# A cross-attention and LoRA-expert kernel: the second tile of the next pair turned in the second joint product instead of in the middle of the third

## The chip, the cores and the metric

The kernel runs on one core of a Trainium2 chip. The metric is the device time of one execution in microseconds (us), as the median of several executions. In the text, PE is the tensor engine, PEld its loads of stationary weights, DVE the vector engine, ACT the scalar engine, POOL the GpSimd engine and SP the sync engine, whose queue issues all DMAs here. PSUM is the memory that PE writes its products to; it is handed out in banks of 128 partitions by 512 float32 numbers.

## The reference

All data are float32. There are 8 batches of 1024 rows, each of 1024 numbers. Two layers follow one another, each with a residual:

```python
# layer 1: attention of layernorm(x) to 64 context rows, masked
scores = einsum('bsd,bmd->bsm', layernorm(x), ctx) / sqrt(1024)
scores = where(mask[:, None, :], scores, -1e30)
readout = einsum('bsm,bmd->bsd', softmax(scores), ctx)
x = x + where(any(mask), readout, 0)
# layer 2: a dense 1024x1024 layer plus 8 low-rank experts, two of them per row
h = layernorm(x)
base = einsum('btd,od->bto', h, weight)
probs = softmax(einsum('btd,ed->bte', h, router_w))
w_dense = the two largest probs of each row, scaled to sum 1, zero elsewhere
Ax = einsum('nd,erd->ner', h, lora_A)                # rank 16
expert_out = einsum('ner,ne,eor->no', Ax, w_dense, lora_B) * 2.0
x = x + base + expert_out
```

## The kernel before

**Tiles and pairs.** A tile is 128 rows of x, so there are 64 tiles and 32 pairs of tiles. Pair u holds tiles r = 0 and r = 1 in `xts[u]`. After `first()`, which does the start and pairs 0 and 1, the function `quad(u)` (L973) is called 15 times, for u = 2, 4, ..., 30. One call does the dense layer and the experts for pairs u and v = u + 1, the second part of the attention for n = u + 2 and m = u + 3 and the first part for f = u + 4. `more` is true while pair n exists (14 calls), `far` while pair f exists (13 calls).

**Turned rows.** For the matmuls the normalised rows h have to stand with their columns on the partitions. `f_rows(u)` (L264) makes h with ACT from two small DVE results; `norm_send` writes it to DRAM (`hd<-h`), `norm_fetch` reads it back in a blocked order into two tiles `hs` (`hs<-hd`), and `rt_turn_tile(u, r)` (L491) turns one of them on DVE, in two instructions of 128x512: one into `hA` (`has[u]`) and one into `hB` (`hbs[u]`). `rt_turn(u)` (L498) does this for r = 0 and r = 1. The tiles `xs`, `xT`, `h` and `hs` share one ring of six buffers (L64).

**Products with fewer multiplications.** The dense layer of a pair is a two-by-two product of blocks (two tiles by two halves of the 1024 columns), done with seven block products and sums of blocks, in the manner of Strassen and Winograd. Four of the seven, numbered 1, 6, 7 and 8, accumulate in one bank (`product`). The other three and a fourth are taken for two pairs at once as "joint" products 5, 3, 2 and 4 (`joint`, L692), each again done with seven smaller products, on quarters of 256 columns. The sums of blocks that these need are made on DVE by `joint_sums`, in two halves `one` and `two`, for joints 5 and 3 together and for joints 2 and 4 together.

**One joint product.** It uses two banks, `jl` (lower: the halves p4 and chain) and `ju` (upper: p2 and p5). PE fills a half bank with a block of four matmuls, DVE adds it to x (`part`, `to_x`; both are line 714 of the profile), and where PE then accumulates further into that half bank it has to wait for DVE's read. The middle of it:

```python
        block(p5, s1, q1, True)          # PE
        part(v, 1, p5)                   # DVE reads p5
        hook(4)
        block(chain, s2, q2, False)      # PE
        part(u, 1, chain)                # DVE reads chain
        hook(5)
        block(p5, s4, b22, False)        # PE goes on in p5
        low(u, p5, 1)
        hook(6)
        block(chain, s3, q3, False)      # PE goes on in chain
        part(v, 0, chain)
```

**Order.** The order of the instructions on PE, DVE, ACT and SP is written by hand: each engine works through its instructions in the order in which the Python code calls them. `hooks` are lists of functions that `joint` calls between its steps, so that other work lies between the blocks. `quad` runs joint 5, 3, 2, 4 at its end. In joint 3, step 2 holds `att_rstd` and `att_exp` of pair f, step 5 `rt_turn(n)` and step 7 `att_divide(f)`. Before joint 2 comes `one` of the sums for joints 2 and 4. In joint 2, step 1 holds `end_3` (the last lora product and add of joint 3) and `f_rows(m)`, step 2 holds `two`, and step 3 `att_turn_p(f)`. In joint 4, step 1 holds `rows_0` (the end of joint 2, stores, `norm_fetch(m)` and a load), and step 5 `rt_sums(n)`, which reads `hA` and `hB` of both tiles of pair n.

Of the kernel before, what the change touches and what calls it, by code (L numbers as in the profile page):

```python
# [24 lines left out]
def kernel(  # L25
# [61 lines left out]
    def transpose_blocked(dst, src):  # L87

        nc.vector.transpose(  # L89
            dst.rearrange("p k (t i) -> p t k i", i=NB),  # L90
            src.rearrange("p t (k i) -> p t k i", i=NB),
        )
# [171 lines left out]
    def f_rows(u: int, fetch: bool = True):  # L264

        nm, std = fts.pop(u)
        rstd = small.tile([P, 2, 1], F32, tag="rstdf", name=f"rstdf_{u}")
        nc.vector.reciprocal(rstd, std)
        nmr = small.tile([P, 2, 1], F32, tag="nmrf", name=f"nmrf_{u}")
        tt(nmr, nm, rstd, ALU.mult)  # L270
        for r in range(2):
            h = ring.tile([P, D], F32, tag="ring", name=f"h_{u}_{r}")
            hss.setdefault(u, []).append(h)
            nc.scalar.activation(  # L274
                h, xts[u][r], AF.Identity, bias=nmr[:, r, :], scale=rstd[:, r, :]
            )
        norm_send(u, fetch)
# [100 lines left out]
    def att_sc(u: int):  # L378
        sc = ps_at.tile([P, 2, M], F32, tag="at", name=f"sc_{u}")
        nc.tensor.transpose(sc.rearrange("p j m -> p (j m)"), scs.pop(u), ident)  # L380
        scs[u] = sc
# [82 lines left out]
    def norm_send(u: int, fetch: bool = True):  # L464

        hds[u] = dram.tile([2 * P, D], F32, tag="hd", name=f"hd_{u}")
        hs_in, hss[u] = hss[u], []
        for r in range(2):
            nc.sync.dma_start(out=hds[u][r * P : (r + 1) * P, :], in_=hs_in[r])
        if fetch:  # L470
            norm_fetch(u)
# [10 lines left out]
    def h_tiles(u: int):  # L482
        has[u] = turned.tile([P, 2, KH, P], F32, tag="hA", name=f"hA_{u}")
        hbs[u] = turned.tile([P, 2, KH, P], F32, tag="hB", name=f"hB_{u}", bufs=3)
# [6 lines left out]
    def rt_turn_tile(u: int, r: int):  # L491
        if r == 0:
            h_tiles(u)
        half = KH * NB
        for t, c in ((has[u], 0), (hbs[u], half)):
            transpose_blocked(t[:, r], hss[u][r][:, :, c : c + half])

    def rt_turn(u: int):  # L498
        for r in range(2):
            rt_turn_tile(u, r)  # L500
# [6 lines left out]
    def rt_low_rank_tile(u: int, r: int):  # L507
        if r == 0:
            pas[u] = ps_rt.tile([P, 2, ER + E], F32, tag="rt", name=f"pa_{u}")
        pa = pas[u]  # L510
        for k in range(KD):
            h = (has[u] if k < KH else hbs[u])[:, r, k % KH, :]
            mm(pa[:, r, :], h, art_sb[:, k, :], start=(k == 0), stop=(k == KD - 1))  # L513
        if r == 1:
            axls[u] = small.tile([P, 2, ER + E], F32, tag="axl", name=f"axl_{u}", bufs=1)
            nc.scalar.copy(axls[u], pas.pop(u))
# [121 lines left out]
    def product(u: int, i: int, between=None, after: int = 0):  # L638

        if i == 1:  # L640
            pps[u] = bank_of(f"b5_{u}") if u < 2 else None, bank_of(f"ch_{u}")
        b5, chain = pps[u]
        if i == 1:
            block(chain, has[u][:, 0], w11, True, between, after)
        elif i == 5:
            block(b5, sms[u][:, 0], t1, True, between, after)
        elif i == 6:
            block(chain, sss[u][1], t2, False, between, after)
        elif i == 7:
            block(chain, sss[u][2], t3, False, between, after)  # L650
        else:
            lora(u, chain, 1, HB, HB)

    def product_add(u: int, i: int):
        b5, chain = pps[u]
        if i == 5:
            add(u, b5, 1, 1)
            add(u, b5, 0, 1)
        else:
            add(u, chain, *{1: (0, 0), 6: (0, 1), 7: (1, 0), 8: (1, 1)}[i])  # L660
# [312 lines left out]
    def quad(u: int):  # L973

        v, n, m, f = [u + i for i in range(1, 5)]
        more = n < NP
        far = f < NP
        b = f // PPB
        new_mem = far and f % PPB == 0

        product(u, 1, (lambda: att_sc(n)) if u == 2 else None, 1)
        pending.pop()()
        product_add(u, 1)
        rt_low_rank_tile(u, 0)
        rt_turn(v)
        product(u, 6)
        if more:
            x_stats(m)
        if u == 2:
            att_divide(n)  # L990
            att_turn_p(n)
        if more:
            att_turn(m)
        product_add(u, 6)
        if u == 2:
            quarter_sums("t4", t4)
        if new_mem:
            mask_bias(b)
            send_mem(b)
        if far:  # L1000
            load_xs(f)
            load_xt(f)
        rt_low_rank_tile(u, 1)
        product(u, 7)
        rt_top(u)
        product_add(u, 7)
        if more:
            att_readout(n)
            att_scores(m)
            rt_turn_low_rank(u)  # L1010
            att_add(n)

        if more:
            product(v, 1, {0: lambda: att_sc(m), 2: lambda: product(u, 8)})
            att_rstd(m)
            att_exp(m)
            one, two = rt_sums_steps(v)
            one()
            product_add(u, 8)
            product_add(v, 1)  # L1020
            two()
            f_sums(n)
            att_divide(m)
            rt_low_rank_tile(v, 0)
            product(v, 6, lambda: att_turn_p(m), 1)
            f_squares(n)
        else:
            rt_sums(v)
            product(v, 1, {0: lambda: rt_turn_low_rank(u), 2: lambda: product(u, 8)})
            product_add(u, 8)  # L1030
            product_add(v, 1)
            rt_low_rank_tile(v, 0)
            product(v, 6)
        if far:
            att_turn(f)
        product_add(v, 6)
        rt_low_rank_tile(v, 1)
        product(v, 7)
        if new_mem:
            turn_mem(b)  # L1040
        rt_top(v)
        if more:
            f_std(n)
            f_rows(n)
        product_add(v, 7)
        one, two = joint_sums(5, u)
        one()
        if more:
            att_readout(m)
        if far:  # L1050
            att_scores(f)
        if u == 2:
            quarter_sums("w21", w21)
        if more:
            rt_turn_low_rank(v)
            att_add(m)
        two()

        def low_v():
            product(v, 8)  # L1060
            product_add(v, 8)

        if more:
            hooks = {2: [low_v]}
        else:
            hooks = {1: [lambda: rt_turn_low_rank(v)], 3: [low_v]}
        if new_mem:
            void_mem(b)
        if far:
            x_sums(f)  # L1070
            x_squares(f)
            x_root(f)
            hooks[3] = [lambda: att_sc(f)]
        end_5 = joint(5, u, hooks)

        hooks = {1: [end_5]}
        if more:
            f_sums(m)
            hooks[5] = [lambda: rt_turn(n)]
        if far:  # L1080
            hooks[2] = [lambda: att_rstd(f), lambda: att_exp(f)]
            hooks[7] = [lambda: att_divide(f)]
        end_3 = joint(3, u, hooks)
        if m + 2 < NP:
            load_xs(m + 2)
            if (f + 2) % PPB == 0 and f + 2 < NP:
                load_mem((f + 2) // PPB)

        one, two = joint_sums(2, u)
        one()  # L1090
        hooks = {1: [end_3], 2: [two]}
        if more:
            f_squares(m)
            f_std(m)
            hooks[1].append(lambda: f_rows(m, False))
        if far:
            hooks[3] = [lambda: att_turn_p(f)]
        end_2 = joint(2, u, hooks)

        def rows_0():  # L1100
            end_2()
            for p in (u, v):
                store(p, 0)
                if not more:
                    store(p, 1, ts(1, HB))
            if more:
                norm_fetch(m)
            if m + 2 < NP:
                load_xt(m + 2)

        hooks = {1: [rows_0]}
        if more:
            hooks[5] = [lambda: rt_sums(n)]
        end_4 = joint(4, u, hooks, not more)

        def last():
            end_4()
            if more:
                for p in (u, v):
                    store(p, 1)  # L1120

        pending.append(last)
# [50 lines left out]
```

## Time and profile before

| what | before |
|---|---|
| median of 3 runs | 1132.66 us (1132.64 to 1134.44) |
| the profiled execution's own time | 1133.88 us |
| its span in the profile | 1132.1 us |
| granted PE clock over the span | 1.00 |
| DMA | 175.73 MB, 155 GB/s on average |
| POOL busy | 1.0 us |

The span is the time from the first to the last recorded instruction of the profiled execution; 1.8 us of its time lie around it. In the profile's rows a name such as `hA<-hs` says which tile is written and which are read, "x4" that four instructions are drawn together, and an L with a number the line of the kernel that issued them. The ends of matmuls are modelled, so their starts are the numbers to trust: a block of four matmuls of 256 columns is judged by the distance to the start of the next one. A bracket at the end of a row of the timeline gives how long the engine was idle before it, and what ended the wait.

The turning instructions of the kernel are these (from the profile's answer for line 89; durations in ns as least, median and most):

```profile
L89 DVE STREAM_TRANSPOSE hA<-hs x60: 668/686/703, 96.8 to 1074.7; 128x512 f32<-128x512 f32 x60
L89 DVE STREAM_TRANSPOSE hB<-hs x60: 668/670/673, 97.4 to 1075.3; 128x512 f32<-128x512 f32 x60
```

### The profile page before, as it was taken

The numbers are of one execution on the slowest core, as the hardware profiler recorded it, in microseconds if no ns is written. First come the engines' busy times: TensorE is split into PE (matmuls) and PEld (weight loads), VectorE is DVE, ScalarE is ACT, GpSimd is POOL, SyncE is SP. The second block draws the span as 40 slices with busy tenths as digits, with TensorE's granted clock in tenths as the row PEclk, the third lists the DMA queues.
The fourth block names the chain that finished last, engine by engine and source line by source line (L and its number), as shares of the span: only waits on it lengthen the run. The fifth ranks groups of instructions, "written<-read, shape, count | busy, mean of one in ns | idle before, by whom it ended". The sixth has DMA issues, their size and how long they took to land.

```text
span 1132.1 us, 15632 instructions
## 1 busy us (share of the span) xinstructions
PE 1117.1 (99%) x5490; PEld 771.2 (68%) x5490; DVE 850.1 (75%) x2099; ACT 553.8 (49%) x1047; POOL 1.0 (0%) x16
## 2 busy tenths in 40 slices
PE   8999999999999999999999999999999999999998
PEld 5555576775867768676685766758677686766767
DVE  6679887777688677886778767787777877867665
ACT  4576563735537354472635736356373544635010
POOL 0000000000000000000000000000000000000000
PEclk9999999999999999999999999999999999999999
DMA  9966256552664726537263474534645554352401
GB/s 215 234 196 196 75 168 194 161 201 97 173 191 120 234 94 174 169 113 260 89 201 120 150 223 130 186 122 155 189 131 186 153 158 155 112 186 75 150 0 75
DMA packets 104462, 175.73 MB, mean 155 GB/s; under 512 B 11904, under 2 KB 76544, under 8 KB 104384
## 3 DMA queue, kind: packets, MB, share of 16 engines
q1 hardware_dynamic: 104384, 174.73, 50.6%
q8 instruction: 43, 0.70, 0.3%
q14 instruction: 35, 0.29, 0.1%
HBM read 107.84 MB, written 66.85 MB: 154 GB/s over the span
## 4 chain that ended last, share of the span: by engine, by line
PE 81%; DVE 11%; DMA 6%; SPq 1%; issue 1%; DVEq 0%
PE ch L631 28%; PE jl L631 12%; PE pa L513 10%; PE ju L631 9%; PE ro L420 5%; PE sct L367 5%; DVE xt L714 3%; PE ju L623 2%; PE ch L623 2%; PE jl L623 2%; DMA mem<-in_ctx_dram 2%; PE plain L631 2%; DVE hA L89 2%; DVE hB L89 1%; DMA xs<-in_x_dram 1%; SPq L83 1%
## 5 line engine op out<-in xcount | busy, mean ns | idle before, releaser
L631 PE MATMUL ch<-t,s 128*128 128x512 f32 x496 | 224.6, 592 | 0.0
L714 DVE TENSOR_TENSOR xt<-jl,xt 128x256 f32<-128x256 f32 (+1 forms) x301 | 139.2, 484 | 112.7 <-PE jl L631 72.5
L193 ACT ACTIVATE junk<-xt 128x1024 bf16<-128x1024 f32 x60 | 63.3, 1055 | 199.7 <-DMA xt<-in_x_dram 198.3
L631 PEld LDWEIGHTS ch<-t,s 128*128 128x128 f32 x496 | 88.5, 190 | 86.1 <-issue 86.1
L631 PE MATMUL ch<-w,hA 128*128 128x512 f32 x248 | 115.9, 593 | 0.0
L714 DVE TENSOR_TENSOR xt<-ju,xt 128x256 f32<-128x256 f32 (+1 forms) x150 | 80.1, 551 | 42.4 <-PE ju L631 41.5
L620 DVE TENSOR_TENSOR xt<-ch,xt 128x512 f32<-128x512 f32 x124 | 85.0, 685 | 33.9 <-PE ch L631 24.5
L274 ACT ACTIVATE h<-xt,nmrf,rstdf 128x1024 f32<-128x1024 f32 x60 | 71.2, 1234 | 52.5 <-DVE nmrf L270 52.5
L620 DVE TENSOR_TENSOR xt<-ro,xt 128x512 f32<-128x512 f32 x128 | 80.4, 683 | 6.0 <-PE ro L420 6.0
L513 PEld LDWEIGHTS pa<-art_sb,hA 128*128 128x128 f32 x512 | 68.5, 190 | 23.2 <-issue 18.9
L631 PEld LDWEIGHTS ch<-w,hA 128*128 128x128 f32 x248 | 44.7, 190 | 43.0 <-issue 42.1
L89 DVE STREAM_TRANSPOSE xT<-xs 128x1024 f32<-128x1024 f32 x60 | 70.5, 1213 | 0.7 <-DMA xs<-in_x_dram 0.7
L513 PE MATMUL pa<-art_sb,hA 128*128 128x136 f32 x512 | 69.9, 279 | 0.0
L202 ACT ACTIVATE junk<-xt,nm 128x1024 bf16<-128x1024 f32 x60 | 68.9, 1148 | 1.9
L513 PE MATMUL pa<-art_sb,hB 128*128 128x136 f32 x512 | 69.7, 279 | 0.0
L253 ACT ACTIVATE junk<-xt,nmf 128x1024 bf16<-128x1024 f32 x60 | 68.7, 1146 | 1.1
L367 PEld LDWEIGHTS sct<-xT,memT_True 128*64 128x64 f32 x960 | 51.8, 137 | 22.7 <-issue 16.7
L513 PEld LDWEIGHTS pa<-art_sb,hB 128*128 128x128 f32 x512 | 64.1, 190 | 0.0
L420 PE MATMUL ro<-mem,pt 64*128 64x512 f32 x256 | 63.6, 615 | 0.4 <-ACT pt L411 0.4
L243 ACT ACTIVATE junk<-xt 128x1024 bf16<-128x1024 f32 x60 | 62.9, 1049 | 1.6 <-DVE xt L620 0.6
L367 PE MATMUL sct<-xT,memT_True 128*64 128x128 f32 x960 | 59.0, 276 | 0.0
L372 ACT COPY scts<-sct 128x128 f32<-128x128 f32 x32 | 8.5, 266 | 102.5 <-PE sct L367 102.5
(183 smaller groups left out, 1852.1 us busy)
## 6 DMA issues: line engine op xcount, KB each, us to landing
xt<-in_x_dram SPq DMA_DIRECT2D x64, 512.0 KB, 6.2
out_dram<-xt SPq DMA_DIRECT2D x62, 512.0 KB, 3.7
xs<-in_x_dram SPq DMA_DIRECT2D x240, 128.0 KB, 3.8
hd<-h SPq DMA_DIRECT2D x60, 512.0 KB, 2.7
hs<-hd SPq DMA_DIRECT2D x240, 128.0 KB, 3.3
mem<-in_ctx_dram SPq DMA_DIRECT2D x16, 256.0 KB, 5.5
w<-in_w_t_dram SPq DMA_DIRECT2D x16, 256.0 KB, 11.5
md<-memc_False SPq DMA_DIRECT2D x7, 256.0 KB, 2.9
```

The costliest lines, as they stand in the source:

```text
L89: nc.vector.transpose(dst.rearrange("p k (t i) -> p t k i", i=NB), src.rearrange("p t (k i) -> p t k i", i=NB),)
L193: nc.scalar.activation(nowhere, xts[u][r], AF.Identity, accum_out=sm[:, r, :])
L202: nc.scalar.activation(nowhere, xts[u][r], AF.Square, bias=stds[u][:, r, :], accum_out=ss[:, r, :],)
L253: nc.scalar.activation(nowhere, xts[u][r], AF.Square, bias=nm[:, r, :], accum_out=ss[:, r, :])
L274: nc.scalar.activation(h, xts[u][r], AF.Identity, bias=nmr[:, r, :], scale=rstd[:, r, :])
L367: mm(sct[r * M : (r + 1) * M, :], mt[:, k, :], x_ts[u][r][:, k, :], start=(k == 0), stop=(k == KD - 1),)
L420: mm(ro, pts[u][rows, :], m[rows, ts(c, HB)], start=True, stop=True)
L513: mm(pa[:, r, :], h, art_sb[:, k, :], start=(k == 0), stop=(k == KD - 1))
L620: tt(xc, bank, xc, ALU.add)
L623: mm(bank, axwts[u][:, r, :], lb_sb[:, c0 : c0 + n], start=alone, stop=True, skip_group_check=True)
L631: mm(bank, a[:, k, :], w[:, k, :], start=(start and k == 0), stop=(k == n - 1), skip_group_check=True)
L714: tt(xc, src, xc, ALU.add)
```

## The change

In the 14 calls of `quad` with `more`, step 5 of joint 3 turns only the first tile of pair n, and the second tile is turned at step 5 of joint 2, which had no hook there. `rt_turn_tile(n, 0)` still sets up `hA` and `hB` for both tiles. No instruction is added, dropped or altered; the order of PE, ACT and SP in the code is unchanged, and only DVE's order differs. `rt_turn` itself stays as it was and is still used elsewhere.

```diff
@@ -1076,7 +1076,7 @@
         hooks = {1: [end_5]}
         if more:
             f_sums(m)
-            hooks[5] = [lambda: rt_turn(n)]
+            hooks[5] = [lambda: rt_turn_tile(n, 0)]
         if far:
             hooks[2] = [lambda: att_rstd(f), lambda: att_exp(f)]
             hooks[7] = [lambda: att_divide(f)]
@@ -1093,6 +1093,7 @@
             f_squares(m)
             f_std(m)
             hooks[1].append(lambda: f_rows(m, False))
+            hooks[5] = [lambda: rt_turn_tile(n, 1)]
         if far:
             hooks[3] = [lambda: att_turn_p(f)]
         end_2 = joint(2, u, hooks)
```

## The prediction

> **What bounds the kernel now.** I read four views in this order: the page's busy times, the list of waits of PE, the chain of waits for one round of the outer loop, and the timelines of PE, of its weight loads (PEld) and of DVE for that same round. First the page:
>
> ```profile
> PE 1117.1 (99%) x5490; PEld 771.2 (68%) x5490; DVE 850.1 (75%) x2099; ACT 553.8 (49%) x1047; POOL 1.0 (0%) x16
> ```
>
> PE is busy nearly all the time, so a change that leaves PE's work alone can gain only in the rest, and only where PE waits. The waits of PE, largest first, begin with one that comes back in every round (us in total, times, longest):
>
> ```profile
> PE ju L631 <- DVE xt L714: 4.7, 13, 0.4
> ```
>
> All 13 lie at one place: PE's timeline has them at 165.72, 234.54, 303.36 and so on to 991.58 us, 68.82 us apart, which is one call of `quad`, always within joint product 2. They belong to the 13 calls with u = 2 to 26, in which `far` holds. I follow the call whose joint 2 begins at 436.48 us; the others show the same offsets to 0.02 us. DVE's timeline (start, duration, then what it waited for in brackets):
>
> ```profile
> 433.10 0.70 DVE L89 STREAM_TRANSPOSE hA<-hs 128x512 f32<-128x512 f32 x1
> 433.73 0.67 DVE L89 STREAM_TRANSPOSE hB<-hs 128x512 f32<-128x512 f32 x1
> 434.32 0.67 DVE L89 STREAM_TRANSPOSE hA<-hs 128x512 f32<-128x512 f32 x1
> 434.91 0.67 DVE L89 STREAM_TRANSPOSE hB<-hs 128x512 f32<-128x512 f32 x1
> 435.51 0.39 DVE L714 TENSOR_TENSOR xt<-jl,xt 128x256 f32<-128x256 f32 x1
> 435.82 0.67 DVE L714 TENSOR_TENSOR xt<-ju,xt 128x512 f32<-128x512 f32 x1
> ...
> 440.53 0.42 DVE L714 TENSOR_TENSOR xt<-ju,xt 128x256 f32<-128x256 f32 x1
> 440.87 0.42 DVE L714 TENSOR_TENSOR xt<-jl,xt 128x256 f32<-128x256 f32 x1
> 443.47 0.42 DVE L714 TENSOR_TENSOR xt<-jl,xt 128x256 f32<-128x256 f32 x1 [2.19 <-PE jl L631]
> ```
>
> From 433.10 to 441.3 no line has a bracket: DVE works off a backlog. The line at 440.53 is `part(v, 1, p5)` of joint 2; it empties the half bank that PE's next block, `block(p5, s4, b22)`, accumulates into. The line at 443.47 is `part(v, 0, chain)`, and before it DVE idles 2.19 us. PE and its loads over the same stretch:
>
> ```profile
> 439.62 1.03 PE L631 MATMUL jl<-w,s_j 128*128 128x256 f32 x4
> 441.01 1.13 PE L631 MATMUL ju<-w,q_j 128*128 128x256 f32 x4 [0.36 <-DVE xt L714]
> 441.97 0.59 PE L623 MATMUL ju<-lb_sb,axwt 128*128 128x256 f32 x2
> ```
> ```profile
> 441.00 0.73 PEld L631 LDWEIGHTS ju<-w,q_j 128*128 128x128 f32 x4 [0.77 <-DVE xt L714]
> ```
>
> A block of four such matmuls takes 0.865 us from start to start where nothing waits (437.35 to 438.21), so the block after 439.62 was due at 440.48. It began at 441.01, 0.53 late, and itself took 0.96 instead of 0.865: **0.63 us lost** (0.53 + 0.10). The bracket shows only 0.36, because the modelled end of the matmul before covers the rest. The load at 441.00 starts 0.47 after the read at 440.53 starts. The same 0.47 stands in joints 3 (431.90, 432.37) and 4 (448.22, 448.69), so this read is the releaser. A second, small loss: the `lora` pair of `end_3` waits for `part(v, 0, chain)` of joint 3 (load at 435.94 after the read at 435.51), and its block takes 0.90 instead of 0.865, 0.035 lost.
>
> **The change, part by part.** Nothing is added or dropped; no DMA moves. Two transposes, `hA<-hs` and `hB<-hs` of the second tile, leave joint 3 after step 5 and enter joint 2 after step 5. On DVE's queue they pass fourteen instructions: the rest of joint 3's reads, `att_divide`, both halves of joint 2's sums, `end_3`'s add, the two small operations of `f_rows`, and three reads of joint 2.
>
> *Taken away in joint 3.* The pair costs 1.19 us start to start (434.32 to 435.51). The next operation can't move up by all of it: `part(v, 0, chain)` needs PE's block that starts at 433.86. A read that waits for a block of four starts 1.06 after the block does (431.70 to 432.76), so at 434.92, and the shift is 435.51 - 434.92 = 0.59. DVE then idles where it had a backlog: what is late next is PE, as it should be. The `lora` of `end_3` is free by then; 0.035 is regained.
>
> *Carried to the read that PE waits for.* From 435.51 to 440.53 DVE runs without a wait, 5.02 us; I add 0.03 because a read that waited is 0.34 ahead of the next and not 0.31 as here. Check of what these operations wait for, at 0.56 earlier: ACT's standard deviation for `f_rows` ends at 436.78 and is wanted at 438.17; the `end_3` bank is complete at about 436.6 and wanted at 437.57; `part(u, 0, chain)` needs the block of 436.48 plus 1.06 = 437.54 and comes at 438.44. So the read of p5 comes at 434.92 + 5.05 = **439.97**. Its other condition, PE's block of 438.75 less 0.035, plus 1.07 as in joint 4 (447.15 to 448.22), gives 439.79, earlier. The sums that the next block needs are complete before the read, in DVE's own order.
>
> *What PE still loses.* The load follows at 439.97 + 0.47 = 440.44. Undisturbed it would start at 440.48 - 0.035 - 0.215 = 440.23 (one matmul ahead). It is 0.21 late. How a late load turns into loss is seen twice: before, 441.00 against 440.27 is 0.73 late for 0.63 lost; in joint 5 (load 425.55 against 425.19, block 425.55 against 425.40 and then 0.96 long) 0.36 late for 0.25 lost. So about 0.10 is covered, and 0.21 late loses about 0.11. Gain per call: 0.63 + 0.035 - 0.11 = **0.55 us**.
>
> *Added in joint 2.* The pair now stands behind `part(u, 1, chain)`, which starts at 439.59 + 1.06 = 440.65. The transposes run from 440.99 to 442.18. By the page "VectorE: DVE Perf Modes", section "The DRAIN you can't avoid", the next operation waits until the pipe is empty, which makes the two durations count in full, 1.37 instead of 1.19, and the end 442.36. The row shows starts 0.59 to 0.63 apart at durations of 0.67 to 0.70, so I take 1.19. Behind them waits `part(v, 0, chain)`, for PE's third block of the chain: with the stall gone that block starts at about 441.86 and the read at 442.92. By row or rule, the pair is hidden in the DVE idle time of 2.19. If this cover were gone, the first to suffer would be the `lora` of `end_2` in joint 4, whose load (444.35, some 0.6 earlier after the change) needs the read to start by about 443.3: another 0.4 of slack. What the moved pair produces is first read by the sums `s<-hA,hB` at 449.42.
>
> *Buffers.* The ring buffer of the second `hs` tile is held until 442.2 instead of 435.5. The next loads through SP, two `hd<-h` at 440.38 and the eight `hs<-hd` from 446.35, could want it; the `xs` loads of this call are issued at 423.73, before the transposes even now. Which buffer they get the trace doesn't show. Cost between 0 and what the first rival below states; I take 0, because the loads into fresh `hs` tiles start 4 us after the release.
>
> *The last call with `more`* (u = 28) has no attention work in these joints. There the block of 1057.07 is followed at 1058.17, 0.24 late, plus the same 0.10 and 0.035. Its read at 1057.70 would move to 1057.27, PE's own limit, and all 0.37 is regained.
>
> **Sum:** 13 x 0.55 + 0.37 = 7.5 us. The profiled execution, 1133.88 us (span 1132.1, 1.8 around it), becomes 1126.4. It lies 1.2 above the median of the runs shown, 1132.66, in which the same stalls occur; from the median: **1125.1 us**.
>
> **A rule that speaks against it.** "Perfetto Trace Analysis", section "Identifying Performance Opportunities", says in substance to work on the most-contended engine. Here that is PE at 99%, and DVE at 75% has room: moving DVE work, with PE's work unchanged, would bring 0 and 1132.7. The rows above show that PE, for all its busy share, loses 0.63 in every call, hidden partly by modelled ends; the section's advice to look for gaps on that engine leads to the same place. I take the rows.
>
> **The rivals.**
> 1. *Slower: a buffer is held too long.* `f_rows(m)` or `norm_fetch(m)` needs the buffer that is now free 6.7 us later (435.5 to 442.2). If that delay passes in full through `hd<-h` to the `hs` loads, they land 6.7 later than 450.4 + 3.3 = 453.7 (issue of the last, and the median to landing), where `rt_turn(v)` wants them at 456.31: 2.6 of slack. DVE's `product_add(u, 6)` behind it, 460.97 for a PE block at 462.04, has about 0.2 (a read of that size takes 0.65, and the load comes 0.2 ahead of its block). PE loses 6.7 - 2.8 = 3.9 per call, against 0.55 gained: + 3.35 x 14 = 47, 1180 us. It undoes the gain from 3.4 us of delay, and is 0.2% slower from 3.5. For it: six ring buffers for four kinds of tile. Against it: SP stands idle from 441.9 to 444.5, and issues these loads only after that.
> 2. *Nothing: the named releaser is not the real one* and PE waits at 441.01 for something that doesn't move, or the pair's place counts for nothing: 1132.7. Against it: the constant 0.47.
> 3. *Half: a wait takes its place.* If DVE, after idling for PE in joint 3, restarts later than 434.92, each 0.1 costs 13 x 0.1 = 1.3 us. A loss of half, 0.28 per call, gives 1132.66 - 3.8 = 1128.9.
> 4. *All of it:* the read comes in PE's own time and nothing is lost: 13 x 0.665 + 0.37 = 9.0, 1123.6.
>
> **How the numbers follow.** Forecast 0.58, rival 1 0.06, rival 2 0.07, rival 3 0.17, rival 4 0.12. About 0.2% (2.3 us) is what a measurement of this kernel can tell from no change; the forecast and rivals 3 and 4 lie beyond it on the fast side: faster 0.87, same 0.07, slower 0.06. The range takes in rivals 3 and 4 with 0.3 for scatter: 1123.3 to 1129.2; rivals 1 and 2, 0.13, are left out.
>
> **What will show it.** Right: `hA<-hs` in pairs, the second directly behind two `part` reads of joint 2; the wait of `ju` for DVE gone from PE's list or under 0.1 each; joint 3's `part(v, 0, chain)` with a bracket naming PE; a call 68.27 us long instead of 68.82. Wrong: a new wait of PE in joint 4 for `part(v, 0, chain)`, a DVE transpose waiting for a DMA at the start of the next call, or the stall in joint 2 at its old size.

## The result, and the profile after

The changed kernel takes 1125.8 us, median of 6 runs (1125.06 to 1128.6), against 1132.98 for the kernel before, also of 6 runs (1132.64 to 1134.44). The ratio is 0.9938, 95% interval 0.9926 to 0.9951: 7.0 us less, between 5.6 and 8.4. The forecast was 1125.1 with a range of 1123.3 to 1129.2.

| | before | after |
|---|---|---|
| median | 1132.98 us | 1125.8 us |
| span of the profiled execution | 1132.1 us | 1123.3 us |
| one call of `quad`, start to start | 68.82 us | 68.28 us |
| weight loads of `ju` waiting for DVE (sum, times) | 16.5 us, 29 | 9.5 us, 28 |

The page after, first the engines, then the head of the chain that ended last, which named PE for 81% and DVE for 11% before:

```profile
PE 1114.2 (99%) x5490; PEld 772.9 (69%) x5490; DVE 853.5 (76%) x2099; ACT 553.3 (49%) x1047; POOL 1.0 (0%) x16
...
PE 97%; DVE 1%; DMA 1%; SPq 0%; ACT 0%; issue 0%; DVEq 0%; ACTq 0%
```

PE's busy share didn't move in the printed percent, although the kernel got 0.6% shorter. The chain is the line that changed: DVE has all but left it. The 13 waits of PE for DVE in joint 2 are gone from the list of PE's waits, where the largest entry that is left is a single 1.6 us at the start. The length of a call is read from the starts of joint 5 in two calls after one another (420.11 and 488.93 us before), 68.28 apart after the change:

```profile
416.56 1.03 PE L631 MATMUL jl<-t,s 128*128 128x256 f32 x4
484.84 1.03 PE L631 MATMUL jl<-t,s 128*128 128x256 f32 x4
```

The call that the prediction followed now runs like this on DVE (the kernel is 4 us ahead here; 435.51 before corresponds to 431.37 after, 440.53 to 436.44):

```profile
429.55 0.70 DVE L89 STREAM_TRANSPOSE hA<-hs 128x512 f32<-128x512 f32 x1
430.18 0.67 DVE L89 STREAM_TRANSPOSE hB<-hs 128x512 f32<-128x512 f32 x1
431.37 0.42 DVE L714 TENSOR_TENSOR xt<-jl,xt 128x256 f32<-128x256 f32 x1 [0.52 <-PE jl L631]
...
436.44 0.42 DVE L714 TENSOR_TENSOR xt<-ju,xt 128x256 f32<-128x256 f32 x1
437.09 0.42 DVE L714 TENSOR_TENSOR xt<-jl,xt 128x256 f32<-128x256 f32 x1 [0.23 <-PE jl L631]
437.43 0.70 DVE L89 STREAM_TRANSPOSE hA<-hs 128x512 f32<-128x512 f32 x1
438.06 0.67 DVE L89 STREAM_TRANSPOSE hB<-hs 128x512 f32<-128x512 f32 x1
439.38 0.42 DVE L714 TENSOR_TENSOR xt<-jl,xt 128x256 f32<-128x256 f32 x1 [0.65 <-PE jl L631]
```

Three brackets tell the story. DVE idles 0.52 us before its restart in joint 3: there is no backlog left. From the restart to the p5 read at 436.44 lie 5.07 us of DVE work; the read behind it already waits 0.23 for PE. And behind the moved pair DVE idles another 0.65 us, so the pair delays nothing. PE's timeline over joint 2, and the weight load that belongs to the block at 436.92:

```profile
436.03 1.03 PE L631 MATMUL jl<-w,s_j 128*128 128x256 f32 x4
436.92 1.13 PE L631 MATMUL ju<-w,q_j 128*128 128x256 f32 x4
437.88 0.59 PE L623 MATMUL ju<-lb_sb,axwt 128*128 128x256 f32 x2
```
```profile
436.91 0.73 PEld L631 LDWEIGHTS ju<-w,q_j 128*128 128x128 f32 x4 [0.26 <-DVE xt L714]
```

The block is due 0.865 after 436.03, at 436.90, and starts at 436.92; it takes 0.96. About 0.12 of the 0.63 us is still lost. No bracket of PE shows it; that of the load names DVE's read, as before.

The span fell by 8.8 us, more than 13 x 0.54 + 0.37 = 7.4. The rest comes from the start of the kernel, which the change doesn't touch: the same transposes `trw` ahead of the first call's joint 5 begin at 143.85 us before and at 142.47 after. In the profiles of the kernels below this point lies anywhere from 142.35 to 144.69. One execution's span is uncertain by so much; the length of a call is not.

### The profile page after: what moved, and what is told of

It is laid out like the page before. It is cut to its first block, busy times and chain, and to the rows that moved or that the text cites. A ratio compares the mean times of both kernels' runs of the same rounds, so it can differ in the third digit from the quotient of the medians.

```text
span 1123.3 us, 15632 instructions
## 1 busy us (share of the span) xinstructions
PE 1114.2 (99%) x5490; PEld 772.9 (69%) x5490; DVE 853.5 (76%) x2099; ACT 553.3 (49%) x1047; POOL 1.0 (0%) x16
## 4 chain that ended last, share of the span: by engine, by line
PE 97%; DVE 1%; DMA 1%; SPq 0%; ACT 0%; issue 0%; DVEq 0%; ACTq 0%
PE ch L631 28%; PE jl L631 18%; PE ju L631 14%; PE pa L513 11%; PE ro L420 5%; PE sct L367 5%; PE ju L623 3%; PE jl L623 3%; PE plain L631 3%; PE ch L623 2%; PE trw L553 1%; PE j L631 1%; DMA w<-in_w_t_dram 1%; DVE xt L620 1%; PE b L631 0%; PE plain L623 0%
```

## The experiments

The diffs are against the changed kernel; the ratios are to the kernel before.

**Adding alone.** The second tile is turned in joint 3 as before, and once more in joint 2.

```diff
-            hooks[5] = [lambda: rt_turn_tile(n, 0)]
+            hooks[5] = [lambda: rt_turn(n)]              # joint 3; joint 2 as after the change
```

> The second tile is turned twice: in joint 3 as before the change, and once more (to the same place, with the same result) in joint 2 after step 5. This is the added half of the change without the removed half. Theory (the new place is hidden in DVE's idle time, the old place costs the stall): stall in joint 2 as before, 0.63 us per call, and the time of before, 1132.7 to 1133.3. Rival (the new place has a price, hidden in the net gain): slower than before, by up to 14 x 1.19 = 17 us if nothing of it is hidden.

Measured: 1132.8 us, ratio to the kernel before 0.9999 (0.999 to 1.0008). The extra pair costs nothing that can be measured: the interval ends at 0.9 us. DVE in joint 2:

```profile
440.51 0.70 DVE L89 STREAM_TRANSPOSE hA<-hs 128x512 f32<-128x512 f32 x1
441.14 0.67 DVE L89 STREAM_TRANSPOSE hB<-hs 128x512 f32<-128x512 f32 x1
442.78 0.42 DVE L714 TENSOR_TENSOR xt<-jl,xt 128x256 f32<-128x256 f32 x1 [0.98 <-PE jl L631]
```

The idle time before the last line, 2.19 us in the kernel before, is 0.98: the pair took its 1.2 out of idle time, and PE's loss of 0.63 per call is there as before (a call takes 68.82 us). So the whole gain comes from the half that is taken away.

**Moved, but ahead of the read.** The second tile is turned at step 3 of joint 2, ahead of the read of p5.

```diff
-            hooks[5] = [lambda: rt_turn_tile(n, 1)]
+            hooks[3] = [lambda: rt_turn_tile(n, 1)]      # att_turn_p(f) stays in step 3 too
```

> The second tile is moved into joint 2 as in the change, but to step 3 instead of step 5, so that it stands on DVE's queue ahead of the read of p5 for which PE waits. Theory (what counts is whether the pair stands before or behind that read): DVE idles in joint 3 for PE as after the change, then carries the 1.19 us to the read, which comes 0.6 later than before the change; PE loses 0.63 + 0.6 = 1.25 per call, 13 x 0.6 + 0.6 = 8.4 us more than before: about 1141. Rival (leaving joint 3 is what counts, whatever the place in joint 2): 1125.8.

Measured: 1141.9 us, ratio 1.0074 (1.0057 to 1.009): slower than the kernel before, by what the theory said. DVE, then PE:

```profile
437.31 0.42 DVE L714 TENSOR_TENSOR xt<-jl,xt 128x256 f32<-128x256 f32 x1 [0.52 <-PE jl L631]
...
442.38 0.70 DVE L89 STREAM_TRANSPOSE hA<-hs 128x512 f32<-128x512 f32 x1
443.00 0.67 DVE L89 STREAM_TRANSPOSE hB<-hs 128x512 f32<-128x512 f32 x1
443.60 0.39 DVE L714 TENSOR_TENSOR xt<-ju,xt 128x256 f32<-128x256 f32 x1
```
```profile
441.96 1.03 PE L631 MATMUL jl<-w,s_j 128*128 128x256 f32 x4
444.04 1.13 PE L631 MATMUL ju<-w,q_j 128*128 128x256 f32 x4 [1.05 <-DVE xt L714]
```

DVE idles the same 0.52 in joint 3 as after the change, and the same work follows; but now the pair stands between it and the read, and costs 1.22 us (442.38 to 443.60). PE starts its block 2.08 after the one before, 1.21 late. Two steps of the hook list separate a kernel 0.6% faster from one 0.7% slower.

**Later still.** The second tile is turned in joint 4.

```diff
-            hooks[5] = [lambda: rt_turn_tile(n, 1)]      # joint 2
...
+            hooks[2] = [lambda: rt_turn_tile(n, 1)]      # joint 4
             hooks[5] = [lambda: rt_sums(n)]
```

> The second tile is turned later still, in joint 4 at step 2, where DVE idles 1.73 us before its read of ju. Its hs buffer is held 5 us longer than after the change, and past the place where the next hs loads ask for buffers. Theory (PE's stall depends on the DVE work ahead of the p5 read alone): as after the change, 1125.8, stall 0.11 per call. Rival (the ring buffer held longer delays the hs or xs loads): a DVE or SP wait for these loads at the start of the next call, up to some 50 us slower in all.

Measured: 1125.41 us, ratio 0.9927 (0.991 to 0.9943), as the changed kernel, with the same 0.12 left on PE's block and the same call of 68.28 us. SP and DVE of this kernel:

```profile
443.08 4.05 SPq L83 DMA_DIRECT2D hs<-hd  x8
```
```profile
443.14 0.70 DVE L89 STREAM_TRANSPOSE hA<-hs 128x512 f32<-128x512 f32 x1
443.76 0.67 DVE L89 STREAM_TRANSPOSE hB<-hs 128x512 f32<-128x512 f32 x1
...
452.45 0.68 DVE L620 TENSOR_TENSOR xt<-ch,xt 128x512 f32<-128x512 f32 x1
453.05 0.70 DVE L89 STREAM_TRANSPOSE hA<-hs 128x512 f32<-128x512 f32 x1
```

The eight loads of the next `hs` tiles are issued while the old tile is still being turned, and the next call's first transpose follows its predecessor without a bracket. A longer hold of the buffer costs nothing here: the first rival of the prediction falls.

**Both tiles late.** The first tile goes to step 5 of joint 2, the second to step 2 of joint 4.

```diff
-            hooks[5] = [lambda: rt_turn_tile(n, 0)]      # joint 3
...
-            hooks[5] = [lambda: rt_turn_tile(n, 1)]
+            hooks[5] = [lambda: rt_turn_tile(n, 0)]      # joint 2
...
+            hooks[2] = [lambda: rt_turn_tile(n, 1)]      # joint 4
```

> First tile at step 5 of joint 2, second tile at step 2 of joint 4, none in joint 3. Theory: the p5 read then comes in PE's own time (DVE no longer carries 1.2 us of the first tile behind its restart), the last 0.11 per call go: 13 x 0.11 = 1.4 us below the changed kernel, 1124.4. Rival (the rest of the stall is PE's own turn-round and not DVE's queue): 1125.8.

Measured: 1125.72 us, ratio 0.9937 (0.992 to 0.9953): as the changed kernel. **This expectation was wrong**, and the trace says why:

```profile
432.17 0.42 DVE L714 TENSOR_TENSOR xt<-jl,xt 128x256 f32<-128x256 f32 x1 [1.73 <-PE jl L631]
...
437.24 0.42 DVE L714 TENSOR_TENSOR xt<-ju,xt 128x256 f32<-128x256 f32 x1
```

With no transposes in joint 3, DVE idles 1.73 us instead of 0.52 and restarts when PE lets it. The read again comes 5.07 after the restart. I had charged the first tile to the way from restart to read, but it stands ahead of the restart, where PE's block covers it. The number alone would also fit the rival that I had named, that the last 0.12 is a turn-round of PE's own; the run with `att_divide` early, below, decides against it.

**Half of the change.** Only the hB transpose of the second tile moves.

```diff
-            hooks[5] = [lambda: rt_turn_tile(n, 0)]
+            hooks[5] = [lambda: rt_turn_tile(n, 0), lambda: rt_turn_half(n, 1, 0)]   # hA, joint 3
...
-            hooks[5] = [lambda: rt_turn_tile(n, 1)]
+            hooks[5] = [lambda: rt_turn_half(n, 1, 1)]                               # hB, joint 2
```

> Half of the change: of the second tile only the hB transpose moves to joint 2, its hA transpose stays in joint 3 behind the first tile. Theory (the shift of the p5 read is capped at 0.59 us by PE's block that part(v, 0, chain) waits for, so one transpose of 0.59 is enough): as the changed kernel, 1125.6, read to stall alike. Rival (each transpose moved is worth its own share of the gain): half the gain, about 1129.3.

Measured: 1125.72 us, ratio 0.9933 (0.9916 to 0.9949): the whole gain for half of the move. DVE in joint 3 reads

```profile
431.48 0.67 DVE L89 STREAM_TRANSPOSE hA<-hs 128x512 f32<-128x512 f32 x1
432.08 0.42 DVE L719 TENSOR_TENSOR xt<-jl,xt 128x256 f32<-128x256 f32 x1
```

with no bracket on the second line: DVE arrives just as PE's block is ready, 0.60 after the transpose began. Of the 1.19 us that the change takes out of joint 3, 0.59 shift the read and 0.6 only lengthen a wait for PE. (The bracket after the change gives 0.52 for that wait, because it counts from the end of the transpose's record, 0.67 long, where the next operation can start after 0.60.)

**Shortening the way from restart to read.** If that is what leaves the last 0.12, then 0.40 us of `att_divide(f)`, moved ahead of the restart into the 0.52 of idle time, must take it.

```diff
-            hooks[7] = [lambda: att_divide(f)]
+            hooks[6] = [lambda: att_divide(f)]           # joint 3, on top of the change
```

> The changed kernel, with att_divide(f) at step 6 of joint 3 instead of step 7, so that its two operations (0.40 us) run in DVE's new idle time of 0.52 us before part(v, 0, chain) instead of behind that read. Theory, corrected after the run with both tiles late: what still delays the p5 read of joint 2 is the 5.07 us of DVE work between its restart in joint 3 and that read; 0.40 less brings the read to PE's own limit and the last 0.11 per call go, 13 x 0.11 = 1.4 us: about 1124.2. Rival (the 0.11 is PE's own turn-round): as the changed kernel, 1125.6.

Measured: 1124.61 us, ratio 0.9922 (0.9905 to 0.9939). Against 1125.8 the median alone would be too little to tell; the trace settles it. DVE, then PE:

```profile
433.09 0.42 DVE L714 TENSOR_TENSOR xt<-jl,xt 128x256 f32<-128x256 f32 x1 [0.15 <-PE jl L631]
```
```profile
437.75 1.03 PE L631 MATMUL jl<-w,s_j 128*128 128x256 f32 x4
438.62 1.03 PE L631 MATMUL ju<-w,q_j 128*128 128x256 f32 x4
```

The blocks of joint 2 stand 0.87 apart, with no loss, and a call is 68.15 us long instead of 68.28. DVE now waits 0.15 before the restart, so `att_divide` did fill idle time.

**Another stall of the same kind.** In joint 5 each read of a half bank is two operations, since its product goes to both tiles of a pair, and PE's block in p5 starts 0.15 late and takes 0.10 longer, before and after, in each of the 12 calls from u = 4 to u = 26. Here other PE work is put between.

```diff
-            hooks = {2: [low_v]}
+            hooks = {5: [low_v]}                         # joint 5, on top of the change
```

> The changed kernel, with the lora product of v (two matmuls of 512 columns, 0.86 us of PE, and its add) in joint 5 moved from step 2 to step 5. Joint 5 loses 0.25 us per call, because the read of p5 is two operations there. Theory (0.86 us of other PE work between the blocks covers it): 14 x 0.25 = 3.5 us below the changed kernel, about 1122.1. Rival (the add of that product, now 0.6 us of DVE work behind the reads, delays DVE in joints 5 and 3 and the stall returns there): 1125.6 or more.

Measured: 1123.09 us, ratio 0.9913 (0.9896 to 0.9929). In joint 5 PE now goes on without a break:

```profile
419.71 1.03 PE L631 MATMUL jl<-t,s_j 128*128 128x256 f32 x4
420.57 1.02 PE L623 MATMUL ch<-lb_sb,axwt 128*128 128x512 f32 x2
421.43 1.03 PE L631 MATMUL ju<-w,q_j 128*128 128x256 f32 x4
```

Each start is 0.86 after the last, and a call takes 68.02 us, 0.25 less than after the change. This holds for 12 of the 14 calls. In the other two, the first (u = 2) and the last (u = 28), PE waits at an earlier place in joint 5, at the block that goes on in chain:

```profile
147.51 1.13 PE L631 MATMUL jl<-t,s_j 128*128 128x256 f32 x4 [1.15 <-DVE xt L714]
```
```profile
1030.72 1.13 PE L631 MATMUL jl<-t,s_j 128*128 128x256 f32 x4 [0.63 <-DVE xt L714]
```

After the change these brackets were 0.30 and none. In these two calls DVE reads chain 2.15 and 1.51 us later than PE's block would let it, and `low_v`, in step 2, had been covering part of that. From joint 5 to the next joint 5 the two now take 69.45 and 60.20 us instead of 68.98 and 59.74, so 0.93 of the 12 x 0.25 = 3.0 is given back. That leaves 2.1 in the profiled executions; the medians differ by 2.7. The expected 3.5 took all calls for equal, and the rival, that the stall returns, came true in two calls, though by the cover that went and not by the add that came.

**Both of these edits.**

> Both of the edits above on top of the changed kernel. Theory: they act at different places and add up, 1.4 + 3.5 = 4.9 us, about 1120.7. Rival (with joint 5 shorter, DVE is late again in joint 2 and one gain eats the other): 1122 to 1124.

Measured: 1121.87 us (1121.43 to 1122.46), ratio 0.9901 (0.9885 to 0.9918), a call 67.90 us long, so 0.38 less than after the change, which is 0.13 + 0.25. In the 12 calls they add up. The first call and that of u = 28 lose again, 0.34 and 0.46 (69.32 and 60.20 us), so the profiled execution gains 3.8 behind the start and the median 3.9, not the expected 4.9. The median lies at the edge of the rival's range, 1122 to 1124, but not for the rival's reason: the blocks of joint 2 stand 0.86 apart (435.08 and 435.94). This is the fastest of the kernels: 11 us below the kernel before, of which 7 come from the change. Of the 28 waits of `ju` loads for DVE that the change left, one is left, of 0.4 us; two waits of PE for DVE on `jl`, 1.8 us in all, are those of the two calls above.

## Why the prediction was right, by its own steps

- *The stall and its size.* 0.63 us per call, with a bracket that shows 0.36: confirmed. The call shortened by 0.54 (68.82 to 68.28), where 0.55 was forecast.
- *The shift is capped by PE.* Forecast: DVE restarts 1.06 after PE's block starts and idles, so 0.59 of the 1.19 count. Confirmed twice, by the 0.52 of idle time after the change and by the half of the change that brings all of the gain.
- *The read after the restart.* Forecast 5.05 us, measured 5.07. The late load and what it costs: forecast 0.11, measured 0.12.
- *The new place is free.* Confirmed by itself, by turning the tile twice. On the price, the trace's 1.19 holds against the 1.37 of the durations in full, which the prediction drew from the page "VectorE: DVE Perf Modes", section "The DRAIN you can't avoid": 1.22 was measured where nothing hid it. The same section adds that an operation that is not held starts earlier, so it does not ask for the full durations everywhere.
- *The last call with `more`.* No loss is left there, as forecast.
- *The advice to work on the busiest engine.* Read as a sum of busy shares it gave 0. It was right to look for gaps on that engine, as "Perfetto Trace Analysis", section "Optimization Strategy", says; they lay in the distance of starts and not in the busy share.
- *The rivals.* A buffer held longer: refuted by the run in joint 4. Nothing: refuted by the result, and by a call that is 0.54 shorter. Half, by a later restart: DVE restarts 1.06 after PE's block, as forecast. All of it: not so, 0.12 is left, and that was the predicted residue. That leaving joint 3 is enough, wherever the pair goes, fell with the run ahead of the read.
- *What was off.* The forecast from the median was 0.7 below the measured one. Part of it is the base: with six runs the median before is 1132.98 and not 1132.66. The rest, 0.4, is less than the runs can tell: the gain lies between 5.6 and 8.4, and 7.5 was forecast. The 8.8 by which the profiled spans differ are no support for the larger size; 1.4 of them lie at the start.

My wrong expectations came after the prediction. In the run with both tiles late it was the same cap forgotten: what stands ahead of a wait that another engine sets is free. In the two runs that move `low_v` I took all 14 calls for equal.

## What to carry to other kernels

Follow the busy engine's stall back along the queue of the engine that releases it, to the last point where that engine itself idles: only the work between that point and the release counts. Taking away more than the engine's wait at that point lets through brings nothing: here 0.59 of the 1.19 us counted. So moved work has to be placed behind the awaited operation, in idle time; whether it stands ahead of that operation or behind it decides the sign. Look also at the first and the last call: a block that is moved to close one gap may have been covering another. Judge a pipelined matmul stream by the distance between starts: 0.63 us was lost where PE's bracket gave 0.36, and 0.12 where PE had none.

## What the runs showed of the hardware

- A weight load that comes late costs its delay less about 0.10 us: 0.73 late lost 0.63, 0.36 late lost 0.25, 0.23 late (load at 436.91 where 436.68 was due) lost 0.12. In the run ahead of the read, 1.43 late (444.04 where 442.61 was due) lost 1.32.
- The hand-over between PE and DVE was the same in every place looked at: DVE's read starts 1.06 to 1.07 us after the start of a block of four 256-column matmuls, and the load that waits for a read of 256 columns starts 0.47 to 0.48 after the read does, 1.53 in all. A block of four takes 0.865, and its first load comes one matmul, 0.216, ahead of it. With one other block between, the load is due 2 x 0.865 - 0.216 = 1.51 after the first block's start. So two blocks in turn are just enough (0.87 apart in the run with `att_divide` early), and two reads instead of one (joint 5, 0.36 late) are not.
